# Eight fused layers on one core: later norms started earlier, zeroing placed by the list, half of the FP4 rounding on GpSimd

## The chip, the cores and the metric

The kernel runs on one core of a Trainium2 chip. The time is device microseconds of one execution; the kernel before takes 1032.96 us (median of three runs, 1032.49 to 1033.01). Work is done by TensorE (PE in the profile, its weight loads PEld), VectorE (DVE), ScalarE (ACT), GpSimd (POOL) and SyncE (SP, which here only issues transfers). Each engine takes its instructions from its own queue strictly in order, so one instruction that waits holds up everything that was put into that queue behind it.

## The reference, cut to what matters

The input x has 4 batches of 512 tokens of 128 numbers, all float32. Eight residual layers follow one another.

```python
x = x + attn_a(norm(x))        # causal softmax attention, 16 heads of 8
x = x + ffn0(norm(x))          # 8 experts, 2 per token, and a shared expert
x = x + attn_b(norm(x))        # linear attention with random features (FAVOR+)
x = x + ffn0(norm(x))          # the same experts again
x = x + gated(norm(x))         # gated linear attention, 8 heads of 64; it norms its input again and adds it back
x = x + ffn1(norm(x))          # gate, up, down with FP4 (E2M1) values in blocks of 16
x = x + retention(norm(x))     # 16 heads of 8, decay per head
x = x + ffn1(norm(x))          # the same FP4 layer again
```

FP4 means: each block of 16 numbers is divided by a sixth of its largest magnitude, rounded to one of 0, 0.5, 1, 1.5, 2, 3, 4, 6 with its sign, and multiplied back. It is done to the layer's input and to the product `silu(gate) * up`, 352 numbers per token.

```python
scale = maximum(max(abs(xb)) / 6.0, 1e-12)
q = GRID[searchsorted(MID, abs(xb / scale))] * sign(xb) * scale
```

The norm is `(x - mean) / sqrt(var + 1e-5)` per token. No layer mixes batches, so one batch can be several layers ahead of another.

## The kernel before, in words

The residual x stays on the chip as `X`, 128 partitions by 16 tiles of 128 tokens, four tiles per batch. Every matrix product goes to one of eight PSUM banks of 128x512 float32. The first layer (about the first 240 us) is written out by hand. Everything after it is a set of streams, one for each batch and stage: `in`, `shared`, `moe`, `total` for the experts (number q counts 0 to 7, two passes over four batches), `inward` and `favor` for the linear attention, `gates`, `keys`, `gated` for the gated layer, then `first` (FP4), `retention`, `leveled` (the group norm and projection of retention) and `second` (FP4).

A planner, the class `Clock`, lays these streams into the four engines' queues when the program is built. A stream is a Python generator: it emits TensorE work directly and hands the work of the other engines to the planner with `later(engine, us, after, do)`, where `us` is the planner's own cost for it and `after` what it depends on. `Clock.steps` repeatedly takes what can start earliest by these costs; at equal times operations of the other engines go ahead of streams, and among streams the one with the larger number in `FAR` goes first. `FAR` therefore decides which of several ready stages gets TensorE. The resulting order in each queue is final; on the chip, semaphores only make instructions wait.

What the change touches, stage by stage:

**Gates** (`gates`, L967). For each batch the norm of the gated layer is computed: `moments` on VectorE (four `bn_stats` and `bn_aggr`, L330 and L331, two tensor_scalars L980 and L981, then the first of three Newton steps of a reciprocal square root begun by two integer operations, L312 and L313), `rest` on GpSimd (the other two steps; with GpSimd all three steps run there as four tiny instructions each, L310), then `centred` (L333): `off = -mean*r`, two GpSimd operations L339 and L340 here, and four ScalarE activations L342 that write `xn`. TensorE turns `xn` (L382), ScalarE copies it with gamma and beta to `xs`, four matmuls with `wa` give the gates, and ScalarE and VectorE make the decays of them: exp, a min (L1008), log, four scans (L1015). `xs`, `D` and `KD` of batches 2 and 3 live in the pool `late`, which takes over the experts' memory. So the streams `gates2` and `gates3` wait for the stream `experts`, which ends the experts when all eight `total`s are emitted.

**The experts' end** (`rest_pools`, L1115). It closes the experts' memory, opens `late`, and calls `rest` (L1545), which loads the retention's constants and zeroes five buffers on GpSimd at that point of the queue: `va` (128x2176, `rv` in the profile) and four masks `ws` (128x1024, `rw`), L1568 and L1569.

**FP4** (`quantized`, L1586). `scales` on VectorE (a block maximum L1594, three small operations L1595 to L1597), a GpSimd multiplication by the reciprocal scale L1610, `power` on VectorE (the exponent bits, L1600), `number` on ScalarE (L1601), `rounded` on VectorE (two scalar_tensor_tensors L1605 and L1606), and a GpSimd multiplication by the scale L1612. In `ffn` (L1616) the product of gate and up is quantized in two halves of 704 numbers per partition, each of two token tiles; `turn` transposes a half on TensorE (L1655), and `down` multiplies it. Two of these layers can be in flight (rooms a and b in names such as `sca` and `scb`), and `retention` has one room, so the four retentions run one after another.

`project` (L1080) ends a gated batch: `centred` on GpSimd and ScalarE, an addition to `X` on GpSimd (L1082), 16 matmuls of `wg` with `D`, and an addition on VectorE (L403).

Of the kernel before, what the change touches and what calls it, by code (L numbers as in the profile page):

```python
# [17 lines left out]
P = 128  # L18
# [21 lines left out]
    "moe": (34,),  # L40
    "shared": (589, 230, 101, 186, 338, 444, 196, 385),
    "total": (34, 334, 167, 440, 467, 482, 19, 193),
    "in": (0, 0, 100, 527, 450, 482, 45, 323),
    "inward": (364, 104, 384, 461),
    "favor": (378, 171, 133, 588),
    "gates": (135, 468, 451, 231),
    "keys": (237, 481, 541, 82),
    "gated": (377, 269, 540, 166),
    "first": (55, 466, 547, 542),
    "retention": (54, 134, 224, 459),  # L50
    "leveled": (326, 293, 76, 394),
    "second": (75, 76, 343, 438),
# [92 lines left out]
class Clock:  # L145
# [13 lines left out]
    def pe(self, us):  # L159
        return self.run("pe", us, self.since)  # L160
# [75 lines left out]
class Net:  # L236
# [667 lines left out]
    def front(self, out):  # L904
# [5 lines left out]
        with ExitStack() as ctx, ExitStack() as now, self.tc.tile_pool(name="kept", bufs=1, space=bass.MemoryType.DRAM) as dram:  # L910
# [58 lines left out]

            def gates(b, clock, gp):  # L970
# [6 lines left out]
                def moments():  # L977
# [4 lines left out]
                    parts.append(self.root_steps(r12[:, b], v, "r12"))  # L982
# [5 lines left out]

                xn = []
                op = later("pool", 2.8, later("dve", 2.1, clock.since, moments), rest)  # L990
                op = later("act", 2.5, op, lambda: xn.append(self.centred(self.new(gp.mid, [P, J, P], "xn"), b, mv[:, b], r12[:, b, 1], own="g")))
                yield [op], "bank"
# [100 lines left out]
            with ExitStack() as over, self.banks():  # L1093
# [8 lines left out]
                known = {}  # L1102
                when = lambda *key: lambda: known.get(key)
# [11 lines left out]
                def rest_pools():  # L1115

                    now.close()
                    gp.late = tp(late, "late", 1)
                    gp.rest = self.rest(over, clock, D, KD, out)
                    clock.run("pool", 5.7, clock.since)  # L1120
                    yield 0.0
# [102 lines left out]
                for b in range(B):  # L1224
                    streams[f"inward{b}"] = ([f"favor{b - 2}"] if b >= 2 else [], None, lambda b=b: into(b), 460)
                    streams[f"favor{b}"] = ([f"inward{b}"], "favor", lambda b=b: featured(b), 400)
                    streams[f"gates{b}"] = (["pools" if b < EARLY else "experts"], None, lambda b=b: gates_of(b), 500 - 10 * b)
# [317 lines left out]
    def rest(self, arm, clock, D, KD, out):  # L1545
# [22 lines left out]
        for t in (va, *ws):  # L1568
            nc.gpsimd.memset(t, 0.0)  # L1569
# [16 lines left out]
        def quantized(dst, src, n, after, own):  # L1586
# [17 lines left out]

                stt(dst, tmp, MAGIC, dst, ALU.add, ALU.add)  # L1605
                stt(dst, tmp, MAGIC, dst, ALU.add, ALU.subtract)  # L1606

            u = n / T
            op = later("dve", 0.8 + 0.7 * u, after, scales)
            op = later("pool", 1.08 * u, op, lambda: nc.gpsimd.tensor_tensor(blk(dst), blk(src), _bc(rc, BLK), ALU.mult))  # L1610
            op = later("act", 0.1 + 0.5 * u, later("dve", 0.42 * u, op, power), number)
# [241 lines left out]
```

## Time and profile before

| What | Value |
|---|---|
| median of three runs | 1032.96 us |
| the profiled execution's own time | 1032.06 us |
| its span, first to last instruction | 1030.3 us |
| TensorE busy in the span | 890.4 us (86%) |
| VectorE, ScalarE, GpSimd busy | 734.2, 560.0, 448.3 us (71%, 54%, 44%) |
| mean granted TensorE clock | 0.940 |
| after the experts' end, 643 to 1026 us: TensorE busy | 291.0 of 383 us |
| from 240 to 643 us: TensorE busy | 375.7 of 403 us |

The profile is of one execution, which was 0.9 us faster than the median. Its own time is 1.8 us more than its span. A busy share says how much of a stretch an engine had an instruction in work; what an engine waited for is in the views of waits and of the timeline, where the bracket behind an instruction gives the idle time before it and what ended it. "Granted clock" is the share of TensorE's full clock that it was given, as the profile shows it.

### The profile page before, as it was taken

The numbers are of one execution on the slowest core, as the hardware profiler recorded it, in microseconds if no ns is written. First come the engines' busy times: TensorE is split into PE (matmuls) and PEld (weight loads), VectorE is DVE, ScalarE is ACT, GpSimd is POOL, SyncE is SP. The second block draws the span as 40 slices with busy tenths as digits, with TensorE's granted clock in tenths as the row PEclk, the third lists the DMA queues.
The fourth block names the chain that finished last, engine by engine and source line by source line (L and its number), as shares of the span: only waits on it lengthen the run. The fifth ranks groups of instructions, "written<-read, shape, count | busy, mean of one in ns | idle before, by whom it ended". The sixth has DMA issues, their size and how long they took to land.

```text
span 1030.3 us, 17949 instructions
## 1 busy us (share of the span) xinstructions
PE 890.4 (86%) x6624; PEld 541.1 (53%) x6624; DVE 734.2 (71%) x1808; ACT 560.0 (54%) x1076; POOL 448.3 (44%) x899
## 2 busy tenths in 40 slices
PE   5999999998999989998988989678798977778734
PEld 3545555554335555444534457446687765566523
DVE  5657777755776898978877755596685864977664
ACT  3556656564774665757476742384345555465422
POOL 2434544341674554555556424463224515343322
PEclk9989999999999999999999999898998997997867
DMA  4000001000000000000000000100000000000000
GB/s 158 2 2 2 2 16 41 2 1 22 0 1 1 1 1 1 2 0 2 11 1 11 1 1 11 32 1 1 1 1 2 1 1 2 1 12 1 12 10 14
DMA packets 8387, 9.82 MB, mean 10 GB/s; under 512 B 1740, under 2 KB 6860, under 8 KB 8036
## 3 DMA queue, kind: packets, MB, share of 16 engines
q1 hardware_dynamic: 8292, 8.60, 2.6%
q8 instruction: 54, 0.88, 0.3%
q14 instruction: 41, 0.34, 0.1%
HBM read 6.50 MB, written 2.10 MB: 8 GB/s over the span
## 4 chain that ended last, share of the span: by engine, by line
PE 53%; DVE 27%; POOL 8%; ACT 7%; issue 4%; DMA 1%; SPq 0%; DVEq 0%; ACTq 0%; POOLq 0%
PE bank L400 48%; DVE D L1015 2%; DVE arg L831 2%; PE bank L382 2%; DVE top L828 1%; DVE h L736 1%; DVE bn L330 1%; DVE D L1606 1%; DVE D L1605 1%; PE bank L1655 1%; DVE top L829 1%; POOL rnt L310 1%; PE bank L492 1%; POOL rstdbe1t L310 1%; DVE den L887 1%
## 5 line engine op out<-in xcount | busy, mean ns | idle before, releaser
L484 DVE TENSOR_REDUCE tops<-bank 128x1 f32<-128x128 f32 (+3 forms) x256 | 110.1, 485 | 55.3 <-PE bank L400 55.2
L400 PE MATMUL bank<-xe,we 128*128 128x512 f32 x256 | 127.6, 620 | 4.5 <-ACT x L737 2.9
L509 ACT ACTIVATE w<-bank 128x512 f32<-128x512 f32 (+1 forms) x192 | 90.5, 526 | 69.5 <-PE bank L400 65.8
L511 POOL TENSOR_SCALAR_AFFINE_SELECT w<-w 128x128 f32<-128x128 f32 x256 | 70.3, 297 | 116.6 <-ACT w L509 116.1
L400 PE MATMUL bank<-qm,kz 32*128 32x384 f32 (+3 forms) x512 | 101.9, 471 | 1.1 <-DVE tops L484 0.6
L400 PE MATMUL bank<-kz,q 32*128 32x512 f32 (+3 forms) x512 | 98.2, 476 | 0.0
L749 POOL TENSOR_TENSOR sum<-sum,y 128x512 f32<-128x512 f32 x56 | 76.7, 1369 | 43.9 <-DVE y L746 41.6
L736 DVE SCALAR_TENSOR_TENSOR h<-h,g 128x512 f32<-128x512 f32 x64 | 60.2, 941 | 21.2 <-ACT g L735 21.1
L400 PEld LDWEIGHTS bank<-xe,we 128*128 128x128 f32 x256 | 43.6, 190 | 49.2 <-issue 29.7
L400 PE MATMUL bank<-h,we 128*128 128x512 f32 x128 | 67.4, 610 | 2.1 <-DVE arg L831 2.1
L735 ACT ACTIVATE h<-bank,half 128x512 f32<-128x512 f32 x64 | 43.8, 684 | 31.6 <-PE bank L400 31.3
L403 DVE TENSOR_TENSOR X<-X,bank 128x512 f32<-128x512 f32 x32 | 21.9, 685 | 50.8 <-PE bank L400 33.0
L400 PE MATMUL bank<-xs,wg 128*128 128x512 f32 x96 | 52.9, 657 | 5.0 <-DVE R L1308 3.3
L400 PEld LDWEIGHTS bank<-kz,q 32*128 32x128 f32 x512 | 38.2, 189 | 32.1 <-issue 11.6
L400 PEld LDWEIGHTS bank<-qm,kz 32*128 32x128 f32 x512 | 47.4, 185 | 13.1 <-DVE tops L484 2.3
L400 PE MATMUL bank<-w,vpad 128*32 128x256 f32 (+3 forms) x512 | 49.0, 449 | 1.8 <-DVE ru L675 1.1
L725 DVE TENSOR_TENSOR xe<-xnT,bank 128x512 f32<-128x512 f32 x64 | 43.2, 678 | 9.9 <-PE bank L400 9.9
L1741 POOL TENSOR_SCALAR_AFFINE_SELECT rw<-rw 128x1024 f32<-128x1024 f32 x32 | 35.4, 1122 | 31.8 <-ACT rw L1740 31.8
L737 ACT ACTIVATE x<-bank,half 128x512 f32<-128x512 f32 x64 | 44.0, 688 | 0.0
L735 ACT ACTIVATE g<-bank,ws 128x512 f32<-128x512 f32 x64 | 43.7, 682 | 0.0
L1740 ACT COPY rw<-bank 128x512 f32<-128x512 f32 x64 | 32.9, 596 | 14.4 <-PE bank L400 14.3
L382 PE MATMUL bank<-ident,xn 128*128 128x128 f32 x80 | 17.5, 314 | 24.9 <-ACT xn L342 19.0
(426 smaller groups left out, 2163.2 us busy)
## 6 DMA issues: line engine op xcount, KB each, us to landing
we<-in_we_dram SPq DMA_DIRECT2D x1, 1536.0 KB, 6.9
wg<-in_wg_dram SPq DMA_DIRECT2D x1, 1280.0 KB, 6.1
X<-in_x_dram SPq DMA_DIRECT2D x4, 256.0 KB, 4.4
kept<-X SPq DMA_DIRECT2D x4, 256.0 KB, 2.5
out_dram<-X SPq DMA_DIRECT2D x4, 256.0 KB, 2.3
wf<-in_wf_dram SPq DMA_DIRECT2D x1, 560.0 KB, 7.5
ws<-in_ws_dram SPq DMA_DIRECT2D x1, 400.0 KB, 4.6
wb<-in_wb_dram SPq DMA_DIRECT2D x1, 320.0 KB, 2.9
```

What stands on the lines that cost most here:

```text
L382: self.nc.tensor.transpose(ps[:, j * P:(j + 1) * P], xn[:, j, :], self.ident)
L400: self.nc.tensor.matmul(out, lhsT=lhsT, rhs=rhs, start=start, stop=stop)
L484: nc.vector.tensor_reduce(top[:, c, 32 * i + r:32 * i + r + 1], ps[i][:, o:o + (c + 1) * P], AX.X, ALU.max)
L509: nc.scalar.activation(w[:, :end], ps[i][:, :end], AF.Exp, scale=scale)
L511: nc.gpsimd.affine_select(out=w[:, o:o + P], in_=w[:, o:o + P], pattern=[[1, P]], compare_op=ALU.is_ge, fill=0.0, base=0, channel_multipli ...
L725: return xe, lambda: tt(xe, xnT[q], ps, ALU.mult)
L735: return (h, x3, lambda: (act(h, ph, AF.Tanh, scale=0.5, bias=half[:, e:e + 1]), act(g, ph, AF.Identity, bias=b1[:, e:e + 1])), lambda: st ...
L736: lambda: stt(h, h, 1.0, g, ALU.add, ALU.mult),
L737: lambda: act(x3, p3, AF.Identity, scale=0.5, bias=half3[:, e:e + 1]))
L749: lambda: nc.gpsimd.tensor_tensor(sums[q], sums[q], y, ALU.add))
L1740: ops = [later("act", 0.6, t, lambda n=n, i=i: nc.scalar.copy(w[n][:, i, :], pp[2 * n + i]), "bank") for i in range(2)]
L1741: ended.append(later("pool", 1.15, ops, lambda flat=flat: nc.gpsimd.affine_select(out=flat, in_=flat, pattern=[[0, 2 * J], [1, P]], compar ...
```

## The change

It has four parts.

1. The streams `gates2` and `gates3` no longer wait for `experts` before they start. Their norm is computed when their batch's second `total` is there; only the step that turns `xn` waits for the experts' end. Batches 0 and 1 keep the GpSimd root; batches 2 and 3 have all three Newton steps and `off` on VectorE. The planner's costs for these operations change with it.
2. The five zeroings become operations of the planner's list, and the copy into `va` waits for them in the plan. The planner's charge of 5.7 us for GpSimd at the experts' end is gone.
3. In the first half of the product of each FP4 layer (`j == 1`), `number` on ScalarE and `rounded` on VectorE are replaced by three GpSimd operations: a tensor_scalar (max with 1, times the constant) and two tensor_tensors (add, subtract), followed by the same scaling as before. The input's quantization and the second halves are left as they were. There are eight first halves (four batches, two layers).
4. All numbers in `FAR` are different.

```diff
 FAR = {
...
-    "gates": (135, 468, 451, 231),
-    "keys": (237, 481, 541, 82),
-    "gated": (377, 269, 540, 166),
-    "first": (55, 466, 547, 542),
-    "retention": (54, 134, 224, 459),
-    "leveled": (326, 293, 76, 394),
-    "second": (75, 76, 343, 438),
+    "gates": (287, 485, 309, 395),
+    "keys": (372, 277, 44, 86),
+    "gated": (276, 383, 205, 372),
+    "first": (5, 509, 269, 371),
+    "retention": (35, 80, 323, 371),
+    "leveled": (206, 143, 94, 307),
+    "second": (78, 244, 77, 265),
 }
...
+            known = {}
+            when = lambda *key: lambda: known.get(key)
...
-                    parts.append(self.root_steps(r12[:, b], v, "r12"))
+                    parts.append(self.root_steps(r12[:, b], v, "r12", eng))
                     next(parts[0])
...
-                xn = []
-                op = later("pool", 2.8, later("dve", 2.1, clock.since, moments), rest)
-                op = later("act", 2.5, op, lambda: xn.append(self.centred(self.new(gp.mid, [P, J, P], "xn"), b, mv[:, b], r12[:, b, 1], own="g")))
-                yield [op], "bank"
+                xn, eng = [], None if b < EARLY else nc.vector
+                op = later("dve", 2.9, clock.since, moments)
+                op = later("pool" if b < EARLY else "dve", 3.0 if b < EARLY else 1.2, op, rest)
+                op = later("act", 2.0, op, lambda: xn.append(self.centred(self.new(gp.mid, [P, J, P], "xn"), b, mv[:, b], r12[:, b, 1], eng, "g")))
+                yield [op, when("experts") if b >= EARLY else 0.0], "bank"
...
-                    clock.run("pool", 5.7, clock.since)
+                    known["experts",] = clock.since
...
-                    streams[f"gates{b}"] = (["pools" if b < EARLY else "experts"], None, lambda b=b: gates_of(b), 500 - 10 * b)
+                    streams[f"gates{b}"] = (["pools"], None, lambda b=b: gates_of(b), 500 - 10 * b)
...
-        for t in (va, *ws):
-            nc.gpsimd.memset(t, 0.0)
+        zeros = [clock.later("pool", 2.0 if t is va else 1.0, clock.since, lambda t=t: nc.gpsimd.memset(t, 0.0)) for t in (va, *ws)]
...
+            scaled = lambda x, by: nc.gpsimd.tensor_tensor(blk(dst), blk(x), _bc(by, BLK), ALU.mult)
+
+            def by_pool():
+                nc.gpsimd.tensor_scalar(tmp, tmp, 1.0, MAGIC, ALU.max, ALU.mult)
+                nc.gpsimd.tensor_tensor(dst, tmp, dst, ALU.add)
+                nc.gpsimd.tensor_tensor(dst, tmp, dst, ALU.subtract)
+                scaled(dst, sc)
+
             u = n / T
             op = later("dve", 0.8 + 0.7 * u, after, scales)
...
-            op = later("act", 0.1 + 0.5 * u, later("dve", 0.42 * u, op, power), number)
-            return later("pool", 1.08 * u, later("dve", 1.36 * u, op, rounded), lambda: nc.gpsimd.tensor_tensor(blk(dst), blk(dst), _bc(sc, BLK), ALU.mult))
+            op = later("dve", 0.42 * u, later("pool", 1.08 * u, op, lambda: scaled(src, rc)), power)
+            if idle:
+                return later("pool", 4.0 * u, op, by_pool)
+            op = later("act", 0.1 + 0.5 * u, op, number)
+            return later("pool", 1.08 * u, later("dve", 1.36 * u, op, rounded), lambda: scaled(dst, sc))
...
-                    halves.append(quantized(hq[:, c], h[:, c], half, ended[-2:], f"{own}{j // 2}"))
+                    halves.append(quantized(hq[:, c], h[:, c], half, ended[-2:], f"{own}{j // 2}", j == 1))
...
-            of_v = later("act", 0.65, pe(0.95), lambda: nc.scalar.copy(of_head.rearrange("p j g i d -> p (j g) i d"), ps1.rearrange("p j (g i d) -> p (j g) i d", i=HG, d=DH)), "bank")
+            of_v = later("act", 0.65, [pe(0.95), *zeros], lambda: nc.scalar.copy(of_head.rearrange("p j g i d -> p (j g) i d"), ps1.rearrange("p j (g i d) -> p (j g) i d", i=HG, d=DH)), "bank")
```

## The prediction

> **What bounds the kernel now.** First I read the busy times by stretch, to see where TensorE is not full. Up to 643 us it is (375.7 of 403 us from 240 us on), so what can be won lies after the experts' end, where it has work in 291 of 383 us. The columns are the stretch, its length, busy time of PE, PEld, DVE, ACT and POOL with instruction counts, and the granted clock.
>
> ```profile
> 643.00:657.00 14.00, 5.85 (x47) 5.14 (x46) 8.73 (x32) 1.65 (x4) 10.59 (x27) 0.87 0.21 58
> 675.00:700.00 25.00, 19.04 (x138) 14.10 (x136) 24.52 (x35) 21.61 (x29) 19.42 (x21) 0.93 0.00 1
> 842.00:855.00 13.00, 4.26 (x27) 3.07 (x26) 10.91 (x50) 5.65 (x12) 0.58 (x1) 0.86 0.00 1
> 879.00:902.00 23.00, 16.78 (x90) 11.32 (x92) 20.89 (x56) 11.56 (x26) 8.94 (x7) 0.93 0.00 0
> ```
>
> TensorE is nearly empty in the first and third; VectorE is full in the second and nearly so in the third and fourth. Then the view of TensorE's waits from 640 us on (in total, times, longest):
>
> ```profile
> PE bank L1655 <- POOL D L1612: 19.0, 6, 7.5
> PE bank L382 <- POOL xna L1612: 14.4, 3, 10.1
> PE bank L382 <- ACT xn L342: 8.9, 1, 8.9
> PE bank L400 <- DVE q L1708: 8.9, 1, 8.9
> ```
>
> The first two are FP4 chains, most of them in the last 50 us, where nothing else is left. The other two are single holes. The timeline shows what makes the first:
>
> ```profile
> 643.32 1.91 POOL L1569 MEMSET rv<- 128x2176 f32 x1 [5.46 <-PE bank L400]
> 645.17 3.70 POOL L1569 MEMSET rw<- 128x1024 f32 x4
> 646.19 0.88 DVE L312 TENSOR_SCALAR r<-v 128x8 uint32<-128x8 uint32 x1
> 649.42 1.65 ACT L342 ACTIVATE res<-X,offp,r 128x128 f32<-128x128 f32 x4 [8.98 <-POOL offp L340]
> 651.16 1.26 POOL L1082 TENSOR_TENSOR X<-X,res 128x512 f32<-128x512 f32 x1 [1.77 <-ACT res L342]
> 656.97 0.22 POOL L340 TENSOR_SCALAR offg<-offg 128x4 f32<-128x4 f32 x1
> 657.23 1.65 ACT L342 ACTIVATE xn<-X,offg,r 128x128 f32<-128x128 f32 x4 [6.15 <-POOL offg L340]
> 657.77 1.63 PE L382 MATMUL bank<-ident,xn 128*128 128x128 f32 x4 [8.92 <-ACT xn L342]
> 660.27 5.33 PE L400 MATMUL bank<-xs,wg 128*128 128x512 f32 x8 [0.87 <-ACT xs L995]
> ```
>
> After the last `total` GpSimd zeroes until 648.9, serves batch 0's projection, and only then begins batch 2's root (652.4 to 656.7). The transposes stand at the head of TensorE's queue meanwhile. After the hole TensorE is slow as well: these transposes take 1.63 us where batch 3's take 0.60, the gate matmuls 5.33 where batch 3's take 3.70. So the hole costs 8.92 + 1.03 + 1.63 = 11.6 us. The second, at 846 us, has the second retention's `q` multiply (L1708) behind two whole norms in VectorE's queue (844.8 to 854.2); 8.85 us, and the scores and state matmuls behind it run 3.1 us longer than the same forms do later (2.09 for 1.17 twice, 1.65 for 0.83, 1.31 for 0.83).
>
> **The change part by part.** I compare the planned orders of both kernels, queue by queue, with durations from the trace. At the last `total` both have given TensorE the same work, except that batch 0's projection (3.74 us) now stands before it.
>
> Norms, roots and zeroing. Batch 2's `xn` is there before the experts end, so its transposes follow at once. Count from TensorE's last experts' matmul. Transposes 0.60, wait for `xs` 0.87, gate matmuls 3.70, then the keys' and values' work 0.55 + 1.05 + 0.49: 7.3 us. Next in TensorE's queue are batch 3's transposes. On VectorE their norm now stands behind the first FP4 norm: residual add 0.69, that norm 1.9 + 12 x 0.2, batch 3's moments 1.9, seven small operations 1.4, block scales 1.5, six root operations 1.2, and then `power` of the FP4 input, which waits for GpSimd. There stand the big memset 1.91, the twelve operations of batch 1's key norms 3.7, four memsets 3.7 and a multiplication 1.06, together 10.4 us, because the memset cannot begin before the experts' memory is free. So `xn` of batch 3 comes from 11.5 to 12.8 us: a new wait of some 5 us. ScalarE then has a rounding step 0.72, a table load 1.28 and a log 1.91 ahead of batch 3's `xs`, which comes at 17.4, when TensorE has been out of work for 2 us. Batch 3's gate matmuls end at 21.1; before, they ended at 674.6, 31.4 us after the last experts' matmul at 643.2, with 3.74 + 1.55 us more work done by then. Won: 31.4 - 5.3 - 21.1 = 5.0 us. Batch 2's log starts some 10 us earlier (14.9 + 3.7 against 29.0), and as VectorE fills the stretch behind it (24.52 of 25 us, mostly scans), up to 10 us can count. I take 7; ends 2, if VectorE gives most back, and 12, the whole hole.
>
> The list. In the new order the second retention's `q` multiply stands ahead of its two norms in VectorE's queue, and a projection, FP4 transposes, an output projection and FP4 products lie before its scores on TensorE. The 8.85 + 3.1 us go. What is late next is the third batch's FP4 chain in front of those scores: about 4 us by my walk along GpSimd (12.5 us of chain against 12.9 us of TensorE work for its first half, and a second half behind it). I take -8; ends -12 and 0. What else the list does has no row: from 240 to 643 us TensorE is idle 27 us, of which the new order could win or add a part. I take 0; ends -5 and +5.
>
> Rounding on GpSimd. Eight times ScalarE loses 0.88 us (L1601) and VectorE 0.89 + 0.89 (L1605, L1606 at their medians): 14.3 us off VectorE. GpSimd gains a tensor_scalar of 704 (0.62 us for 512 at L837, so 0.85) and two tensor_tensors of 704. Their nearest rows are the scaling with a broadcast operand at the same size, 1.39, and the full addition of 512 at L1082, 1.27, so 1.74; I take the second. 0.85 + 3.48 = 4.3 us (ends 3.6 and 4.6), 35 us in all. The chain of a first half grows by 4.3 - 2.66 = 1.6 us. Most first halves are covered: before, the first one was ready at 704.0 and used at 713.2. The last one is not. GpSimd takes both halves' first multiplication, then the three new operations (1015.3 to 1019.6), then both scalings; the first transposes move from 1018.7 to 1021.1 and the end by 2.4 us. Against that, the last retention's group norm loses the first half's 2.9 us (979.76 to 982.63) in front of it on VectorE. Net 0.
>
> But GpSimd also holds VectorE up, as here:
>
> ```profile
> 905.02 2.14 POOL L1741 TENSOR_SCALAR_AFFINE_SELECT rw<-rw 128x1024 f32<-128x1024 f32 x2 [0.74 <-ACT rw L1740]
> 905.11 1.02 DVE L318 SCALAR_TENSOR_TENSOR grstd<-grstd1t,grstd 128x1 f32<-128x1 f32 x1
> 906.16 1.01 DVE L316 SCALAR_TENSOR_TENSOR grstd1t<-grstd 128x1 f32<-128x1 f32 x1
> 907.21 0.16 DVE L310 TENSOR_TENSOR grstd1t<-grstd1t,grstd1v 128x1 f32<-128x1 f32 x1
> ```
>
> Operations of 0.16 us take 1.0 while GpSimd masks. From 902.89 to 907.16 VectorE loses 2.0 us against 3.5 us of GpSimd work, 57%. If all 35 us met such work, VectorE would lose 20 us and win 14.3. As much of its work shows no such stretch (block maxima keep 0.89 us beside GpSimd at 1012), I take the two as even: 0; ends -10 (VectorE's relief counts in the stretches 879 to 946, where it is the fuller engine) and +19 (rival 1).
>
> The Trainium skill speaks against this part. "SBUF — State Buffer", section "Who interferes with whom", says that a VectorE instruction with two SBUF inputs and a GpSimd instruction that reads SBUF exclude one another for the whole instruction. The rows above agree. By that rule alone, with every new GpSimd operation facing such an instruction, the sum would be 35 - 14 = 21 us worse on VectorE than mine.
>
> The sum: 1032.06 (the profiled execution's own time) - 7 - 8 + 0 = 1017.1. The median is 0.9 above that execution, so 1018 us.
>
> **The rivals.**
> 1. GpSimd becomes the brake. The new operations lie on the path at all eight places (8 x 1.6 = 13 us), and VectorE loses 57% of 35 us while it wins 14.3 (+6): 19 us on top of the rest, 1037 us. For it: retention's masks wait in the same GpSimd queue. Against it: GpSimd is busy in 147 of the last 383 us, and the new order has the added operations mostly between two retentions. It turns the change slower when about seven of the eight places cost their full 2.4 us, or earlier if the holes do not close.
> 2. Only the experts' end is won; another wait takes the place of the `q` multiply: 1033 - 7 = 1026 us.
> 3. No change that can be measured: VectorE swallows the early start in 675 to 700 us and the FP4 chain the other: 1032 us.
> 4. VectorE's relief counts on top: 1018 - 10 = 1008 us.
>
> **How the numbers follow.** Chances: forecast (1012 to 1023) 0.40, rival 1 0.20, rival 2 0.22, rival 3 0.06, rival 4 0.12. Faster by over 0.2% (about what a measurement can tell from no change) are forecast, 2 and 4: 0.74; same 0.06; slower 0.20. The range goes from 1006 (rival 4 with a good list) to 1037 (rival 1), which leaves out about 0.15.
>
> **What would show it.** Right: no wait of 9 us before `ident,xn`, a wait of about 5 us before batch 3's instead; no wait for `q` before the second retention's scores; GpSimd some 35 us busier and VectorE some 12 less; a first-half rounding of 4 to 4.6 us. Wrong: small VectorE operations of 1 us and more behind L1611 to L1613, TensorE waiting for masks (L1741 before), or a stretch before the last `total` that is longer by more than 4 + 5 us.

## The result, and the profile after

The changed kernel takes 1034.31 us (median of 15 runs, 1029.22 to 1039.74) where the kernel before takes 1032.96 (15 runs beside them, 1030.42 to 1033.64). The ratio is 1.0018, with a 95% interval of 1.0005 to 1.0031: no change by the bound of 0.2%, and if anything a small loss. 1018 was forecast. The execution profiled of the changed kernel took 1029.99 us, 4.3 us less than its median, so its trace shows where time lies rather than the whole of the loss. The runs below were taken in several rounds, in which the kernel before took 1031.9 to 1033.3 us; each ratio is against the kernel before of the same round. The difference of two medians and that of their ratios can be apart by up to 2.4 us, so differences of 1 to 2 us are not to be relied on.

Busy time by stretch (columns: stretch, length, TensorE, its weight loads, VectorE, ScalarE, GpSimd with counts, then the granted clock), first before, then after:

```profile
640.00:690.00 50.00, 36.59 (x233) 25.87 (x232) 35.13 (x81) 30.10 (x46) 25.98 (x50) 0.90 0.07 20
840.00:1028.00 188.00, 125.72 (x1198) 95.91 (x1197) 124.99 (x354) 84.68 (x183) 67.04 (x55) 0.81 0.02 7
```

```profile
640.00:690.00 50.00, 34.86 (x181) 22.86 (x183) 40.94 (x93) 31.57 (x46) 26.26 (x39) 0.80 0.06 17
840.00:1028.00 188.00, 118.82 (x1138) 90.37 (x1132) 133.72 (x332) 75.28 (x171) 96.86 (x68) 0.77 0.02 7
```

Around the experts' end (640 to 690 us) TensorE has less work than before, not more, and VectorE has 5.8 us more. From 840 us on GpSimd has 29.8 us more, and VectorE, from which the roundings were taken, 8.7 us more. TensorE's waits of the changed kernel from 640 us on (in total, times, longest):

```profile
PE bank L1665 <- POOL D L1608: 36.0, 6, 12.3
PE bank L400 <- POOL rw L1751: 11.3, 6, 5.8
PE bank L382 <- ACT xn L342: 9.2, 1, 9.2
```

The wait for the second retention's `q` is gone. The FP4 chains wait 36.0 us, where `POOL D` had 19.0 and `POOL xna` 14.4; the masks of the retention wait 11.3 us, which had no such row; and the hole before `xn`, 8.9 us, is 9.2 us in front of batch 3's transposes. The retentions' first scores come at 748.4, 833.5, 890.5 and 938.0 us (before: 785.0, 855.1, 901.6, 945.7), the last addition at 1022.95 (1025.07): a lead of 37 us on the first retention is 2 us at the end. Most of that lead was no gain, only another order, which leaves other stages' work for later: at 785 us TensorE had been busy for 721.5 us, only 8.2 more than before (713.3).

### The profile page after: what moved, and what is told of

It is laid out like the page before. It is cut to its first block, busy times and chain, and to the rows that moved or that the text cites. A ratio compares the mean times of both kernels' runs of the same rounds, so it can differ in the third digit from the quotient of the medians.

```text
span 1028.2 us, 17939 instructions
## 1 busy us (share of the span) xinstructions
PE 886.6 (86%) x6624; PEld 536.7 (52%) x6624; DVE 749.7 (73%) x1812; ACT 553.2 (54%) x1068; POOL 486.9 (47%) x895
## 4 chain that ended last, share of the span: by engine, by line
PE 53%; DVE 27%; POOL 9%; ACT 6%; issue 4%; DMA 0%; SPq 0%; DVEq 0%; ACTq 0%; POOLq 0%
PE bank L400 48%; DVE arg L831 2%; DVE top L828 2%; DVE bn L330 1%; POOL D L1608 1%; PE bank L382 1%; DVE h L736 1%; DVE den L887 1%; PE bank L1665 1%; DVE X L403 1%; DVE top L829 1%; POOL D L1613 1%; POOL fwa L1611 1%; DVE mvb L331 1%; PE bank L492 1%
## 5 line engine op out<-in xcount | busy, mean ns | idle before, releaser
L749 POOL TENSOR_TENSOR sum<-sum,y 128x512 f32<-128x512 f32 x56 | 78.8, 1407 | 61.5 <-DVE y L746 59.4
L736 DVE SCALAR_TENSOR_TENSOR h<-h,g 128x512 f32<-128x512 f32 x64 | 63.7, 998 | 8.7 <-ACT g L735 8.6
L1665 PE MATMUL bank<-ident,D 128*128 128x128 f32 (+1 forms) x96 | 19.7, 359 | 42.4 <-POOL D L1608 36.0
L400 PE MATMUL bank<-xs,wg 128*128 128x512 f32 x96 | 50.7, 636 | 3.4 <-DVE D L1082 2.5
```

Source lines behind the costliest of these rows:

```text
L400: self.nc.tensor.matmul(out, lhsT=lhsT, rhs=rhs, start=start, stop=stop)
L736: lambda: stt(h, h, 1.0, g, ALU.add, ALU.mult),
L749: lambda: nc.gpsimd.tensor_tensor(sums[q], sums[q], y, ALU.add))
```

## Experiments

### The parts, alone and together

Three edits can be made apart: the list (the numbers in `FAR`; only two zeros in its row `in` stay), norms with planned zeroing, and rounding. Every kernel here is planned anew, so its queues differ from the others'.

The list alone:

```diff
 FAR = {
-    "moe": (34,),
+    "moe": (135,),
...
```

> The kernel before with the new numbers in FAR as its only edit. Prediction's step B and the trace: the 8.9 us wait for the retention's q and some 5 us of TensorE idle before the experts' end go, 1020 to 1026 us. Rival (the numbers fit only the kernel with the other edits, since the planned costs differ): 1031 us or more. If the norms' and zeroing's kernel changes nothing and this one does, the 6 us by which norms, zeroing and list together are faster than before come from the list.

1022.01 us, ratio 0.9908 (0.9891 to 0.9924), as expected. Half of that is won before the experts' end, where TensorE was busy for 375.7 us in the kernel before:

```profile
240.00:643.00 403.00, 380.46 (x2021) 203.12 (x2022) 310.30 (x621) 241.41 (x426) 203.32 (x354) 0.99 0.01 4
```

Behind it the wait for the second retention's `q` is gone, but 3.5 us for the third's, 8.3 us for `V` (L1288) and 15.0 us for `one` (L1068) have come in.

Norms and zeroing with the old list, and no rounding on GpSimd:

> The kernel before with the early norms (batches 2 and 3 rooted on VectorE) and the planned zeroing; the old list FAR, rounding as before. Prediction's step A: 7 us less, 1025 us. Rival (from the changed kernel's trace: the hole only moves in front of batch 3's transposes, because the memsets and the FP4 norm hold VectorE there, and the stretch from the last total to the second FP4 products is no shorter): within 1030 to 1036 us.

1039.62 us, ratio 1.0077 (1.0060 to 1.0094): outside both. In this kernel TensorE does have more work in 640 to 690 us (40.3 for 36.6 us), as the prediction's step has it; the time is lost behind, in an order laid out anew, where the 8.9 us for `q` stand as before and waits of 7.4, 5.6 and 4.9 us (two together) have come in. Why that order is bad was not followed further.

Rounding alone, with the old list:

```diff
-                    halves.append(quantized(hq[:, c], h[:, c], half, ended[-2:], f"{own}{j // 2}"))
+                    halves.append(quantized(hq[:, c], h[:, c], half, ended[-2:], f"{own}{j // 2}", j == 1))
```

> The kernel before with GpSimd rounding of the first halves as the only edit (the list FAR, the norms and the zeroing of before). Theory (rounding costs some 20 us by itself): 1045 to 1058 us. Rival (it costs only in the new order, where it meets the retention's masks): within 1030 to 1037 us. Eight first halves at 3.3 to 4.1 us more on their own chain would be 26 to 33 us at most if none were covered.

1034.29 us, ratio 1.0022 (1.0011 to 1.0033): the rival's figure.

The changed kernel without rounding (the same line the other way round):

> The changed kernel with its norms, zeroing and list, but every first half rounded by ScalarE and VectorE as before. Theory (rounding): the profile of the changed kernel has its first retention's scores 21 us earlier than before and loses it all from there to the end, where the GpSimd rounding lies. Without it those 18 to 21 us stay: 1011 to 1018 us. Rival (list): the new order packs the last 190 us worse by itself: 1028 us or more. Rival (half and half, GpSimd's share hidden where GpSimd is otherwise idle): 1020 to 1026 us.

1026.07 us, ratio 0.9934 (0.9915 to 0.9953): 8.2 us less than the changed kernel, at the edge of the second rival. (The 21 us that the expectation names are the second retention's lead; the first's is 37.)

List and rounding, without norms and zeroing:

> The kernel before with the new list and GpSimd rounding of the first halves, without the early norms and the planned zeroing. Rounding cost 2.3 us with the old list and norms (1034.3 for 1032.0) and 8.2 us with the new ones (1034.3 for 1026.1). Theory (the new list has less idle time to cover it): list alone plus 6 to 9 us, 1028 to 1031 us. Rival (it is the early norms that it meets): 1023 to 1025.5 us.

1038.85 us, ratio 1.0063 (1.0043 to 1.0084): 16.8 us more than the list alone, beyond what was expected.

| list | norms, zeroing | rounding | us | ratio |
|---|---|---|---|---|
| old | | | 1032.96 | 1 |
| new | | | 1022.01 | 0.9908 |
| old | yes | | 1039.62 | 1.0077 |
| old | | yes | 1034.29 | 1.0022 |
| new | yes | | 1026.07 | 0.9934 |
| new | | yes | 1038.85 | 1.0063 |
| new | yes | yes | 1034.31 | 1.0018 |

The list is the only part that gains by itself. Rounding costs time wherever it is added: 2.3, 8.2 or 16.8 us. Norms with zeroing cost 7.6 us with the old list and 4.1 with the new one (there the two intervals overlap a little), but beside rounding they win 4.5 us (1034.31 for 1038.85). So what a part costs depends on the rest; each of these kernels has another order.

### What an operation of the rounding costs

Behind the end of the kernel before, GpSimd does a list of operations on 128x704 float32, three of each, with VectorE idle, then beside VectorE operations of two inputs, then beside such of one input.

```diff
+            gp.tensor_scalar(pb, pa, 1.0, MAGIC, ALU.max, ALU.mult)
...
+            gp.tensor_scalar(pb, pa, 1.0, MAGIC, ALU.mult, ALU.add)
...
+            gp.tensor_scalar(pb, pa, MAGIC, None, ALU.mult)
...
+            gp.tensor_tensor(pd, pb, pc, ALU.add)
```

> The kernel before, and behind its end a list of GpSimd operations on 128x704 float32, three times each, first with VectorE idle, then beside VectorE operations of two SBUF inputs, then beside VectorE operations of one input. The time has no meaning but for the added rows. Theory (the form costs): tensor_scalar with max and mult takes 2.5 us with VectorE idle too, and mult with add 0.85. Rival (contention): it takes 0.85 with VectorE idle and 2.5 only beside it. For the tensor_tensors of 704: 1.65 to 1.75 alone, and up to 2.2 beside VectorE; a VectorE operation of two SBUF inputs goes from 0.9 to 2.2 us beside GpSimd, one of one input stays as it is.

The timeline of it, alone: L1842 is max and mult, L1846 mult and add, L1850 a single mult, L1852 the addition; then L1842 and L1852 beside VectorE's two-input operations.

```profile
1032.11 7.86 POOL L1842 TENSOR_SCALAR pb<-pa 128x704 f32<-128x704 f32 x3 [8.87 <-DVE pb L1836]
1047.99 2.50 POOL L1846 TENSOR_SCALAR pb<-pa 128x704 f32<-128x704 f32 x3
1056.71 6.07 POOL L1850 TENSOR_SCALAR pb<-pa 128x704 f32<-128x704 f32 x3
1062.87 5.15 POOL L1852 TENSOR_TENSOR pd<-pb,pc 128x704 f32<-128x704 f32 x3
1078.35 9.71 POOL L1842 TENSOR_SCALAR pb<-pa 128x704 f32<-128x704 f32 x3
1116.08 6.46 POOL L1852 TENSOR_TENSOR pd<-pb,pc 128x704 f32<-128x704 f32 x3
```

A third of each: 2.62 us for max and mult, 0.83 for mult and add, 2.02 for a single mult, 1.72 for the addition. The first three run beside VectorE's memsets until 1036.4, but mult and max, with VectorE idle, takes 2.62 too (L1844, 7.85 for three). It is the form, as the theory had it. Row L837, from which 0.85 us was worked out, is mult and add. In the changed kernel the three operations take 2.57 + 1.66 to 2.07 + 1.67 to 2.20 us, 5.9 to 6.8 in all and 6.0 to 7.0 with the gaps.

VectorE's rows of the same list: three operations of two inputs and three of one input alone, then 48 and 60 of them beside GpSimd.

```profile
1073.00 2.74 DVE L1859 SCALAR_TENSOR_TENSOR vc<-va,vb 128x704 f32<-128x704 f32 x3
1075.78 1.65 DVE L1861 TENSOR_SCALAR vc<-va 128x704 uint32<-128x704 uint32 x3
1078.30 58.37 DVE L1864 SCALAR_TENSOR_TENSOR vc<-va,vb 128x704 f32<-128x704 f32 x48 [0.87 <-POOL pa L1862]
1137.33 53.21 DVE L1869 TENSOR_SCALAR vc<-va 128x704 uint32<-128x704 uint32 x60
```

The 48 should take 43.8 us and take 58.4; the 60 should take 33.0 and take 53.2. So I was wrong that one input goes free: it loses 20 us against 47 us of GpSimd's work, more than the operations of two inputs (15 against 50). GpSimd's 21 operations rise from 39.8 to 49.7 and 47.2 us. The page "SBUF — State Buffer", section "Who interferes with whom", of the Trainium skill has a line for each kind: it also counts the two-port modes of `tensor_scalar` among what can contend with GpSimd. I had drawn only on its sentence about two inputs. That L1861 runs in such a mode no run here shows; that it loses time beside GpSimd these rows do.

These are means over all of GpSimd's forms, and the form decides here too. While GpSimd adds (6.46 us from 1116.08 on), VectorE gets through some 3.1 operations of two inputs, 2.1 us each, the longest 2.24; while it does max and mult (9.71 us from 1078.35 on) some 9.0, 1.08 us each, and five of the eight that lie wholly in it take 0.89, as alone. With one input it is 1.8 us beside the additions (the longest 1.87) and 0.78 beside max and mult (counts and means worked out from the starts in the trace). So the exclusion for the whole instruction, as I gave that page in the prediction, is not what the rows of max and mult show: GpSimd reads SBUF in these as well. By this list, what holds VectorE in the new rounding is above all the two tensor_tensors.

### Rounding: the instructions, or the order laid out for them

The changed kernel in its own order, but the old instructions emitted where GpSimd would begin:

```diff
             def by_pool():
-                nc.gpsimd.tensor_scalar(tmp, tmp, 1.0, MAGIC, ALU.max, ALU.mult)
-                nc.gpsimd.tensor_tensor(dst, tmp, dst, ALU.add)
-                nc.gpsimd.tensor_tensor(dst, tmp, dst, ALU.subtract)
+                number()
+                rounded()
                 scaled(dst, sc)
```

> The changed kernel with its order of work on every engine kept as planned for GpSimd rounding; only, where GpSimd would begin its three new operations, the old one is put into ScalarE's queue and the two old ones into VectorE's. This parts the instructions from the order that was planned with them. Theory (the instructions cost the time: 5.9 to 6.8 us of GpSimd for what took 2.7, and VectorE held up): 1011 to 1019 us. Rival (the order costs it, since the planner counts 5.5 us of GpSimd and puts other work first): 1028 us or more.

1030.19 us, ratio 0.9972 (0.9952 to 0.9991): 4.1 us less than the changed kernel, but in the range of the rival. The same edit in the kernel with list and rounding:

> The new list with GpSimd rounding planned (1038.9 us), every queue in that order, but the old instructions of ScalarE and VectorE in place of GpSimd's three. The list alone, in its own order, takes 1022.0. Theory (instructions and order take some half each, as with the early norms, where the same step brought 4.1 of 8.2 us): 1030 to 1034 us. Rival 1 (only the instructions): 1021 to 1025 us. Rival 2 (only the order): 1036 us or more.

1034.76 us, ratio 1.0030 (1.0016 to 1.0043), 4.1 us less than with GpSimd's instructions; between the theory and rival 2. So far this reads as if the order were the larger cost. The reverse edit answers that: the order planned for the old rounding, with GpSimd's instructions put into it.

```diff
-            if idle:
-                return later("pool", 4.0 * u, op, by_pool)
-            op = later("act", 0.1 + 0.5 * u, op, number)
+            op = later("act", 0.1 + 0.5 * u, op, None if idle else number)
+            op = later("dve", 1.36 * u, op, None if idle else rounded)
...
+            return later("pool", 1.08 * u, op, by_pool if idle else lambda: scaled(dst, sc))
```

> Norms, zeroing and list changed, in the order planned for the old rounding (1026.1 us); GpSimd's three operations stand where GpSimd scales the rounded first half, and ScalarE's and VectorE's old ones are left out. TensorE's queue is the same. Theory (the instructions cost some 4 us, the order the rest): 1029 to 1031.5 us. Rival 1 (all is the instructions' doing in any order that does not plan for them): 1033 us or more. Rival 2 (free in this order): 1025 to 1027.5 us.

1054.88 us, ratio 1.0201 (1.0176 to 1.0226). With the list alone:

> The list alone, in the order planned for the old rounding (1022.0 us), with GpSimd's three operations put into it in the same way. Planned for, the same instructions gave 1038.9. Theory (order is most of it): 1024 to 1028 us. Rival (the instructions are): 1033 us or more.

1050.86 us, ratio 1.0177 (1.0155 to 1.0199). Both are 28.8 us more than the same order with the old rounding (1026.07 and 1022.01), 3.6 us for each of eight first halves. The rivals were right. TensorE's waits from 640 us show it, the list alone first, then with GpSimd's instructions in its order:

```profile
PE bank L1655 <- POOL D L1612: 21.1, 7, 8.3
```

```profile
PE bank L1667 <- POOL D L1608: 48.5, 10, 11.2
```

27.4 us more of one wait: little covers the rounding there. Not all of it is the length of the instructions. They stand where the scaling stood, and at two places with the norms, and at one without, GpSimd begins them only 3.5 to 7.7 us after `power`, where in the changed kernel it is 1.3 us at most. The order planned for GpSimd wins back 20.6 of 28.8 us with the norms, and 12.0 without, which I put down to other work of TensorE in front of the transposes; but with the old instructions in it that order is 4.1 and 12.7 us slower than the one planned for them. How much of these is the order alone isn't shown: at four of the eight first halves ScalarE's step stands late in its queue there and begins 1.0 to 3.0 us after `power`, against 0.7 at most in the order planned for it with the norms.

The list with the memsets moved (below), with GpSimd rounding by a cheaper form at all places but the last:

```diff
+                number()
+                nc.gpsimd.tensor_scalar(tmp, tmp, 1.0, MAGIC, ALU.mult, ALU.add)
```

> The list alone with the memsets behind the first FP4 input (1019.3 us), its order kept; the first halves rounded by ScalarE and GpSimd with the mult and add form, except the very last one, which stays as before. VectorE loses 7 times 1.8 us. Theory (seven of eight places are covered): 1017 to 1020.5 us. Rival (GpSimd holds VectorE up for more than it relieves it of): 1022 us or more.

1047.08 us, ratio 1.0142 (1.0120 to 1.0165): 27.8 us more, the rival's side. It doesn't judge the form: ScalarE's step was emitted at the place of GpSimd's, late in ScalarE's queue, and GpSimd waits for it from 2.1 to 4.5 us at three places.

### The form, and the last place

The changed kernel in its order, with ScalarE's old step and the form of 0.83 us:

```diff
-                nc.gpsimd.tensor_scalar(tmp, tmp, 1.0, MAGIC, ALU.max, ALU.mult)
+                number()
+                nc.gpsimd.tensor_scalar(tmp, tmp, 1.0, MAGIC, ALU.mult, ALU.add)
```

> The changed kernel with every queue in its order, but in the first halves ScalarE does its old step (0.88 us), and GpSimd's tensor_scalar is the form mult and add, which the priced list had at 0.83 us alone for 2.62 of max and mult. GpSimd loses 8 times 1.7 us, the chain of a first half 0.9 us. Theory (the price of that form is the mis-sized term, and the chains that set the end go through it): 1 us for each of the two or three places that TensorE waits at, 1030.5 to 1032.5 us. Rival (the two tensor_tensors and VectorE's hold-up cost it, not this form): 1033.5 us or more.

1028.93 us, ratio 0.9975 (0.9956 to 0.9995), 5.4 us less: more than the theory. And only the very last first half rounded as before:

```diff
             def by_pool():
-                nc.gpsimd.tensor_scalar(tmp, tmp, 1.0, MAGIC, ALU.max, ALU.mult)
...
+                if idle == 2:
+                    number()
+                    rounded()
```

> The changed kernel in its own order on every queue; only the first half of the very last FP4 layer (batch 3) is rounded by ScalarE and VectorE where GpSimd would begin. The changed kernel's last transposes wait 12.3 us for GpSimd (before: 7.5). Theory (at this place nothing covers it): the wait goes to 7.5 us and the time by 4 to 5 us, 1029 to 1031 us. The prediction had 2.4 us here: 1032 us. Rival (the second half then ends last): 1033.5 us or more.

1030.19 us, ratio 0.9979 (0.9960 to 0.9998), 4.1 us less, as the theory had it. That is as much as all eight first halves brought above (1030.19): in sum the other seven bring nothing in this order. Whether they are covered, or the late steps of ScalarE eat what they would bring, these runs don't tell. The last first half in the changed kernel (L1611 to L1613 are the new operations):

```profile
1005.96 1.62 POOL L1608 TENSOR_TENSOR D<-KD,rcb 128x704 f32<-128x704 f32 x1 [1.04 <-DVE scb L1598]
1007.56 2.55 POOL L1611 TENSOR_SCALAR fwb<-fwb 128x704 f32<-128x704 f32 x1
1010.20 1.87 POOL L1612 TENSOR_TENSOR D<-fwb,D 128x704 f32<-128x704 f32 x1
1010.58 2.24 DVE L1606 SCALAR_TENSOR_TENSOR D<-fwb,D 128x704 f32<-128x704 f32 x1
1012.15 2.19 POOL L1613 TENSOR_TENSOR D<-fwb,D 128x704 f32<-128x704 f32 x1
1014.42 2.73 POOL L1608 TENSOR_TENSOR D<-D,scb 128x704 f32<-128x704 f32 x2
1015.86 1.54 PE L1665 MATMUL bank<-ident,D 128*128 128x128 f32 x6 [12.33 <-POOL D L1608]
```

and with that one half rounded as before:

```profile
1005.92 1.63 POOL L1608 TENSOR_TENSOR D<-KD,rcb 128x704 f32<-128x704 f32 x1 [1.05 <-DVE scb L1598]
1007.26 1.04 DVE L1605 SCALAR_TENSOR_TENSOR D<-fwb,D 128x704 f32<-128x704 f32 x1 [0.95 <-ACT fwb L1602]
1008.33 0.89 DVE L1606 SCALAR_TENSOR_TENSOR D<-fwb,D 128x704 f32<-128x704 f32 x1
1009.37 1.53 POOL L1608 TENSOR_TENSOR D<-D,scb 128x704 f32<-128x704 f32 x1 [1.82 <-DVE D L1606]
1010.96 1.54 PE L1669 MATMUL bank<-ident,D 128*128 128x128 f32 x6 [7.47 <-POOL D L1608]
```

Both begin within 0.05 us of each other; the transposes come 4.9 us later with GpSimd's three operations. In the first fence VectorE's L1606 belongs to the second half and takes 2.24 us beside L1612, where it takes 0.89 without.

### The experts' end

The changed kernel without rounding on GpSimd (1026.07 us), with the five memsets behind the second multiplication of the first FP4 input in GpSimd's queue; the other queues are the same.

```diff
-        zeros = [clock.later("pool", 2.0 if t is va else 1.0, clock.since, lambda t=t: nc.gpsimd.memset(t, 0.0)) for t in (va, *ws)]
+        zeros = [clock.later("pool", 2.0 if t is va else 1.0, clock.since) for t in (va, *ws)]
+        unset = [va, *ws]
...
+            def last():
+                scaled(dst, sc)
+                while unset:
+                    nc.gpsimd.memset(unset.pop(0), 0.0)
```

> Norms, zeroing and list changed, rounding as before (1026.1 us), with every queue in the same order but for the five memsets, which stand behind the second multiplication of the first FP4 input in GpSimd's queue. In the kernel without this move the tiny VectorE operations of batch 3's root (two tensor_scalars, two integer operations) take 0.9 to 1.0 us beside the memsets (2.8 us in the changed kernel), against 0.2 otherwise, 2.9 us in all. Theory (memsets hold VectorE, and that chain sets the wait before batch 3's transposes): those four take 0.2 each, the wait shrinks from 8.9 to 6 us, the time by 2 to 3 us: 1023 to 1024.5 us. Rival (the memsets hold up what then runs on VectorE): the wait shrinks and the time stays, 1025 to 1028 us.

1023.00 us, ratio 0.9909 (0.9893 to 0.9926), 3.1 us less: the theory, though the intervals overlap a little. The changed kernel's timeline shows what the memsets do:

```profile
644.87 3.63 POOL L1570 MEMSET rw<- 128x1024 f32 x4
645.70 2.83 DVE L983 TENSOR_SCALAR v<-gmvx 128x4 f32<-128x4 f32 x1
645.77 2.76 DVE L984 TENSOR_SCALAR v<-gmvx 128x4 f32<-128x4 f32 x1
648.57 0.17 DVE L312 TENSOR_SCALAR r<-v 128x8 uint32<-128x8 uint32 x1
651.34 0.69 DVE L1595 TENSOR_REDUCE scb<-xnb 128x32 f32<-128x512 f32 x1 [1.71 <-ACT xnb L342]
654.73 0.15 DVE L336 SCALAR_TENSOR_TENSOR offg<-gmvx,r 128x4 f32<-128x4 f32 x1
655.47 1.63 PE L382 MATMUL bank<-ident,xn 128*128 128x128 f32 x4 [9.21 <-ACT xn L342]
```

Two VectorE operations on four numbers take 2.8 us and end with the last memset, at 648.5; with the memsets moved they take 0.17 and 0.16. After that batch 3's root (L312 to L336) is split: its first step is done at 649.5, then VectorE waits 1.7 us for the FP4 input and makes its scales (L1595), and the root ends at 654.9.

The memsets in one block, where they stood before:

> New list and early norms, rounding as before, but the five memsets where they stood before, in one block at the experts' end, with the old planned charge; all queues but GpSimd's are in the order of the kernel with planned zeroing (1026.1 us). The block then ends before batch 3's root and meets the first FP4 norm instead. Theory (a memset holds VectorE's tensor_scalars wherever it meets them): some 3 us are lost at the FP4 norm and the keys' norms instead, 1025 to 1028 us. Rival (the planned place is the fault): 1022 to 1024 us.

1028.10 us, ratio 0.9946 (0.9924 to 0.9967), against 1026.07: at the upper end of the theory, though the intervals overlap. Three operations of the first FP4 norm's root (L297, L312, L313) take 2.3 us beside the block for 0.5. The old place is no better, so the planned one is not the fault. Now batch 3's whole norm ahead of the first FP4 norm:

```diff
-                op = later("dve", 2.9, clock.since, moments)
-                op = later("pool" if b < EARLY else "dve", 3.0 if b < EARLY else 1.2, op, rest)
+                if b < EARLY:
+                    op = later("pool", 3.0, later("dve", 2.9, clock.since, moments), rest)
+                else:
+                    op = later("dve", 4.1, clock.since, lambda: (moments(), rest()))
...
-            op = later("dve", 4.5, clock.since, moments)
+            op = later("dve", 4.5, clock.since + (4.0 if unset else 0.0), moments)
```

> Norms, zeroing and list changed, rounding as before, memsets behind the first FP4 input (1023.0 us), and batch 3's whole gate norm planned ahead of the first FP4 norm on VectorE. In the kernel without this step TensorE waits 6.5 us for batch 3's xn, because VectorE computes the FP4 norm (4.2 us) and waits for its input in between. Theory (that queue order is what kept the hole open): the wait falls to some 2 us and the time by 3 to 4 us, 1019 to 1020.5 us. Rival (ScalarE and VectorE then hold TensorE up behind the gates, at the log and the scans): the wait falls and the time stays within 1021.5 to 1024 us.

1028.55 us, ratio 0.9961 (0.9948 to 0.9975): 5.6 us more, worse than the rival. TensorE's waits from 640 to 700 us, first without this step, then with it:

```profile
PE bank L382 <- ACT xn L342: 6.5, 1, 6.5
PE bank L400 <- DVE V L1290: 4.4, 3, 2.2
PE bank L400 <- DVE D L1082: 2.3, 1, 2.3
```

```profile
PE bank L400 <- DVE KD L1660: 4.6, 1, 4.6
PE bank L382 <- ACT xn L342: 2.9, 1, 2.9
PE bank L400 <- DVE V L1292: 2.3, 2, 2.0
PE bank L382 <- POOL xnb L1611: 1.5, 1, 1.5
```

The hole does shrink by 3.6 us, and the FP4 layer that was pushed back opens others: the FP4 input comes 1.5 us late, and matmuls behind that layer wait 4.6 us for VectorE's step on the gate (L1660). From there on the two kernels have nearly the same waits, only later (the second retention's `rn` transposes at 797.82 and 801.60 us, the last addition at 1015.86 and 1021.50).

The memsets moved in the list alone, with no early norms:

```diff
-        for t in (va, *ws):
-            nc.gpsimd.memset(t, 0.0)
+        unset = [va, *ws]
```

> The new list alone (1022.0 us) with the five memsets moved behind the second multiplication of the first FP4 input, every other queue as it is there. Theory (memsets hold VectorE and GpSimd's own root of batches 2 and 3 wherever they stand at the experts' end): the list-alone kernel has an 8.3 us hole there too, and 2 to 4 us go: 1018 to 1020 us. Rival (that hole is set by something else, the keys' norms or the copy of V): 1021.5 to 1023 us. Set against norms, zeroing and list with the memsets moved (1023.0): if this one is faster by more than 2 us, the early norms cost time by themselves; if it is equal, they are worth nothing here.

1019.26 us, ratio 0.9858 (0.9834 to 0.9883), the theory: faster than either kernel, and 3.7 us below the same thing with early norms (5 by the ratios). Last, the changed kernel with the memsets moved and the form of 0.83 us:

> The changed kernel with both mendings: the mult and add form in the first halves (5.4 us less alone) and the memsets behind the first FP4 input (3.1 us less alone, without GpSimd rounding). Theory (two separate costs at two places): both add up, 1025 to 1027 us, faster than before by half a per cent. Rival (the later waits swallow the earlier gain): 1028 to 1030 us.

1029.12 us, ratio 0.9963 (0.9944 to 0.9982), no less than with the form alone (1028.93, ratio 0.9975) by anything that these runs can tell: the rival's figure. The hole before batch 3's transposes does shrink, from 8.8 to 6.5 us; that later waits swallow it is argued, not shown.

## Why the prediction was wrong

By its own steps it had -7 for the experts' end, -8 for the list, 0 for rounding. Taken one after another (list, then norms and zeroing, then rounding), the runs show -10.0 (1022.0 for 1032.0), +4.1 and +8.2. With rounding ahead of norms and zeroing it is -10.0, +16.8 and -4.5: the shares of the last two depend on the sequence, their sum of 12.3 us doesn't.

**The list: right in size, only in part by its terms.** -8 was forecast for it and 10 measured; the 8.9 us for the second retention's `q` are gone. But "What else the list does has no row" was 0 with ends of 5 us, and 4.8 us more of TensorE's work done by 643 us came from just there (380.5 for 375.7), while behind it the list alone has waits of 15.0 and 8.3 us that no term had. That the sum came out near is partly luck. The "about 4 us" of FP4 chain that I saw in front of those scores did not come there (they wait 0.4 us); it came behind them.

**The experts' end: no 7 us, and without rounding the sign was wrong.** The step was "Won: 31.4 - 5.3 - 21.1 = 5.0 us", then "up to 10 us can count. I take 7", with 2 as the poorest end. It saw that batch 3's norm would stand behind the FP4 norm and priced "a new wait of some 5 us"; it was 9.2, of which some 2.5 us are VectorE's operations held up by the memsets (L983 to L312 take 2.9 us for 0.3; moving the memsets took the hole from 8.8 to 6.5). The larger mistake, as I read it, is that a hole in TensorE's row is time that can be had. The run with the norm first, planned anew too, closed more than half of that hole and lost 5.6 us: VectorE is busy in 40 of the 50 us from 640 to 690 and carries the FP4 norm, the gate norm and the scans, each needed by TensorE soon after. The row for that was in my own view: 24.52 of 25 us of VectorE from 675 us on. That VectorE's order, not its amount of work, sets the stretch is argued from these runs and not measured by itself. Why norms and zeroing win 4.5 us beside rounding stays open.

**Rounding: "I take the two as even: 0" failed**, by two terms. The first is the price: "a tensor_scalar of 704 (0.62 us for 512 at L837, so 0.85)" was worked out from another form, and max with mult takes 2.57. The three operations take 5.9 to 6.8 us for 4.3 (ends 3.6 and 4.6), the chain grows by 3.2 to 4.2 us and not by 1.6, and the last place costs 4.9 us of waiting and 4.1 of time where I had 2.4. The second is "Most first halves are covered". In the two orders that don't plan for it the time grows by 28.8 us, 3.6 for each of the eight on average, part of it for the place in GpSimd's queue. In the changed kernel's order the last place alone costs as much as all eight, but that order takes 4.1 us more than the one planned for the old rounding even with the old instructions in it. So the cover has to be made by the planned order, and it seems to cost order elsewhere; I priced an edit that the planner sees as if the planner would do the rest as before. The masks point the same way: TensorE waits for them 11.3 us in the changed kernel, 13.0 with the old instructions in its order and 7.3 in the order planned for those, so it is the order, not GpSimd's load, that makes it wait.

VectorE's side was nearer. The changed kernel keeps VectorE busy for 749.7 us, the same without GpSimd's rounding for 745.2: with 14.3 us of work taken away it is 4.5 busier, so 18.8 us are lost to GpSimd's 48.4 more (486.9 for 438.5). I had put the loss at 20 us at most and then took 14.3. The rate of 57% came from masks and scalings; in the list of single operations the additions cost VectorE far more than max and mult does.

**The rivals.** Rival 1 (GpSimd the brake at all eight places) had the mechanism; with the right price its size is what the two orders not planned for it show (28.8 us), while in the changed kernel rounding costs 8.2. It was left at 0.20 because "the new order has the added operations mostly between two retentions", which is true and, as I read it, is what was paid for. The time of rival 3 came out, for other reasons: not two small changes, but 10 us won and 12 lost.

**What was to show it.** The wait before batch 3's transposes was there (9.2 for 5 us), GpSimd was 38.6 us busier (35 forecast), VectorE not 12 us less busy but 15.5 more, a first half's rounding longer than 4.6 us, and of the signs against me two came: VectorE operations stretched beside L1611 to L1613 and TensorE waiting for masks.

## What to carry to other kernels

Price an operation that is new on an engine from a row of the same form, not of the same size: here max with mult took three times what mult with add took. Where a planner orders the work, an edit costs what the new order costs, so test it three ways: planned for, in the old order, and its order with the old instructions. And a hole of one engine need not be worth its length: ask whether the engine that ends it has idle time to give. Here, moving work forward on a busy VectorE moved the hole.

## What the hardware showed that I had not expected

- GpSimd's tensor_scalar of 704 numbers takes 0.83 us as mult and add, but 2.02 with one operation alone (max or mult) and 2.62 with max and mult (or mult and max).
- Four memsets by GpSimd, which read nothing, hold VectorE's tensor_scalars on four numbers to 2.8 us, or to 0.9 to 1.0 us each, one for each memset.
- VectorE's one-input operation of 704 numbers goes from 0.55 to about 0.95 us beside GpSimd, a larger share than the two-input one (0.91 to about 1.29). These are means; beside GpSimd's additions alone it is about 1.8 and 2.1 us, beside max and mult about 0.78 and 1.08.
- The kernels in the new list's order planned for GpSimd rounding spread over 7 to 10 us in 8 to 15 executions; the kernel before spread over 3 to 7 us in 7 to 23, the others over 3 to 7 in 4 to 10. In the changed kernel's runs the time goes roughly with the granted clock: the four fastest (1029.2 to 1031.2 us) had 0.937 to 0.945, the four slowest (1035.7 to 1039.7) 0.927 to 0.929, but two at 0.937 took 1035.1 and 1035.2. What moves the clock was not followed.
